# Gram matrix and moments of q and k as blocks of 32 channels on the diagonal, four products at once in strips of array columns

## The chip, the cores and the metric

The kernel runs on one core of a Trainium2 chip, in float32 throughout. The metric is the device time of one execution in microseconds (us). The program is one launch that chains four layers. The change touches only the first part of the first layer, called the preparation, which takes about the first 454 us of the span.

A core has TensorE for matrix products (PE in the profile; its weight loads are listed apart as PEld), VectorE (DVE), ScalarE (ACT), GpSimd (POOL), and SyncE (SP), which issues most of the transfers. TensorE reads SBUF and writes PSUM. A product has a stationary operand, `lhsT`, and a moving operand, `rhs`, and computes `lhsT.T @ rhs`. In this trace each float32 product appears as two passes on PE, each with a weight load of its own on PEld; a transpose appears as one pass.

## The reference

The input `x` has 2 images of 128 channels and 128 x 128 pixels. The first layer is an axial attention along columns, with batch normalisations whose statistics come from the data:

```
x = x + _L0_conv_ref(_gn(x), ...)          # _gn: group norm, groups of 4 channels
...
xg = x.reshape(NW, 8, C // 8, H)            # NW = 2*128 sequences, 8 groups of 16 channels
qkv = einsum('bgch,gdc->bgdh', xg, wg)      # 32 outputs a group: 8 q, 8 k, 16 v
qkv = _bn(qkv, g_qkv, b_qkv, (0, 2), ...)   # moments of each of 256 outputs
q, k, v = qkv[:, :, :8], qkv[:, :, 8:16], qkv[:, :, 16:]
qr = einsum('bgci,cij->bgij', q, q_emb)
kr = einsum('bgci,cij->bgij', k, k_emb).swapaxes(2, 3)
qk = einsum('bgci,bgcj->bgij', q, k)
stacked = _bn(concatenate([qk, qr, kr]), g_sim, b_sim, (0, 2, 3), ...)   # 24 channels
```

The kernel needs the moments of `qkv` and of the three kinds of logits before it can do the attention, and gets them without forming the logits. All of them follow from second moments of channels, and only between channels of one group: the groups of `xg` hold 16 channels each and those of q and of k hold 8 each. So only blocks on the diagonal of each matrix of second moments are used. In `qk` the mean square of the logits is the sum over channel pairs of (second moments of q) times (those of k), sequence by sequence; in `qr` and `kr` it is the sum of second moments at a position times a table made from the embeddings.

## The kernel before

`layer0_prepare` (line 92) has three stages, one after the other. The engines PE, DVE and ACT are driven through `InOrder`, a recorder that keeps the instructions in the order in which the program gives them; all such instructions carry line 81 in the profile, so they are told apart by their tiles. GpSimd and single instructions of the short parts between the stages carry their own lines.

**Gram stage.** `load_image` (line 859) issues 16 transfers of 1 MB on SP, 8 for each image, into `xa[n]` (128 channels on partitions, all pixels of an image behind each other). For every image, 32 steps `t` of 4 image rows follow. `turn(n, t)` transposes the 4 rows (4 transposes of 128 x 128 into one PSUM tile `ps_x`, of which there are three) and copies the result to one of three tiles `xt`, ACT for even `t` and DVE for odd. `xt` has 129 columns per row: 128 channels and a column of ones, so that the product also gives sums. `gather(n, t)` then multiplies each of the 4 turned rows with itself: 4 products with 128 weights and 129 moving columns, all summed in one PSUM tile `gram[n]`. The loop is software-pipelined by one: `turn(t + 1)` is issued ahead of `gather(t)`. Meanwhile GpSimd works through the embedding table (lines 174 to 183), which is needed only in the third stage.

**Between Gram and the second stage** (lines 192 to 301) a serial chain of small instructions on ACT, DVE and PE turns the Gram matrices into group norm scales and the scaled weights `wz`. It uses the whole 128 x 128 matrix `gx` as weights in one product for each image, against weights that are zero outside each channel's own group.

**Second stage, `sequences` and `moments`.** 64 steps, 4 columns of the image each. `sequences(i)` makes q, k and v for 4 columns: 4 products with 128 weights and 256 moving columns into two tiles `ps_zb`; DVE adds the shifts and writes q and k to `zb` (in two blocks, q with 64 channels and k with 64, each with a 65th column of ones) and v to `vs`, which SP stores every fourth step. `moments` of the step before is issued behind that: 8 products with 64 weights and 65 moving columns, written to PSUM partitions 0 to 63 or 64 to 127, so that two neighbours sit in two different halves of the array's columns. ACT copies the q part out (`gq`), DVE multiplies it by the k part, GpSimd adds it to `acc`.

**Third stage, `positions`, `project` and `against_embeddings`.** 32 steps `t` of 4 image rows. `positions(t)`: 8 products with 128 weights and 128 moving columns into two tiles `ps_zt`; DVE writes q and k to `zt`, again in blocks of 65. From `t = 4` on, two or three `project` calls follow (each one product with 512 moving columns into `ps_q`, then two ACT instructions into `sa` and `sb`), and SP stores `sb` (1 MB, tensor `qb_d`) and `sa` (2 MB, `qa_d`) when they are full. `against_embeddings(t - 1)` is last: 16 products with 64 weights and 65 moving columns in the two halves into `pg`; DVE multiplies by the table (`prod`), GpSimd adds to `acc`.

At the end of the second and the third stage a short chain (`logit_scales`) sums `acc` under the mask `strip`. Then `layer0_attention` begins, whose first loads read `qb_d`, `qa_d` and `v_d` back from memory.

The attention itself, which the change does not touch, has products in quarters of the array's columns: `embedded_pe` writes 16 outputs with 32 moving columns to PSUM partitions 0, 32, 64 and 96 in turn (tiles `po<-et,ve`), and `values` does the same with 128 moving columns (`po<-et,vt`).

Of the kernel before, what the change touches and what calls it, by code (L numbers as in the profile page):

```python
# [7 lines left out]
F32 = mybir.dt.float32  # L8
# [7 lines left out]
P = 128  # L16
N = 2
# [74 lines left out]
def layer0_prepare(env, x, prm, mem, alphas):  # L92
# [9 lines left out]
    with ExitStack() as ctx:  # L102
# [13 lines left out]
        with ExitStack() as early:  # L116
# [20 lines left out]

            xt = [wp.tile([P, RT, P + 1], F32, name=f"xt{j}", tag=f"xt{j}") for j in range(3)]
            for t in xt:
                nc.gpsimd.memset(t[:, :, P : P + 1], 1.0)  # L140
            gram = [
                pp.tile([P, P + 1], F32, name=f"gram{n}", tag=f"gram{n}") for n in range(N)
            ]
# [45 lines left out]
            count = float(S * S)  # L189
            gx = wp.tile([P, N, P + 1], F32, name="gx0", tag="gx0")  # L190
            dg = wp.tile([P, P], F32, name="diag", tag="diag")
            mx = wp.tile([P, N, 2], F32, name="mx", tag="mx")
            for n in range(N):
                nc.scalar.mul(gx[:, n], gram[n], 1.0 / count)
                nc.vector.tensor_tensor(dg, gx[:, n, 0:P], env.ident, ALU.mult)
                nc.vector.tensor_reduce(mx[:, n, 1:2], dg, AX.X, ALU.add)
                nc.vector.tensor_copy(mx[:, n, 0:1], gx[:, n, P : P + 1])
            ps = pp.tile([P, 2 * N], F32, name="psg_l0", tag="ps_small")
# [127 lines left out]
        def along(n, k, shape):  # L326
            return (
                rows[:, k, 1 + n, :]
                .rearrange("p (b c) -> p b c", b=(2, NG)[k])
                .unsqueeze(1 if k == 0 else 2)  # L330
                .to_broadcast(shape)
            )
# [3 lines left out]
        onto = kp.tile([P, 1 + N], F32, name="onto", tag="onto")  # L336


        with ExitStack() as part:
            sp = part.enter_context(tc.tile_pool(name="l0s", bufs=1))  # L340
            gp = part.enter_context(tc.tile_pool(name="l0g", bufs=2))
            pp = part.enter_context(tc.tile_pool(name="l0pm", bufs=2, space=PSUM))
            acc = sp.tile([P, 2, 65], F32, name="acc2", tag="acc2")
            nc.gpsimd.memset(acc, 0.0)
            zb = [sp.tile([P, RT, 2, 65], F32, name=f"zb{j}", tag=f"zb{j}") for j in range(2)]
            for t in zb:
                nc.gpsimd.memset(t[:, :, :, 64:65], 1.0)

            def sequences(i, vs):
# [3 lines left out]
                for hf in range(2):  # L353
                    ps = pp.tile([P, 2, 2, P], F32, name="ps_zb", tag="ps_zb", bufs=4)
                    for j in range(2):
# [7 lines left out]
                    dve.tensor_tensor(  # L363
                        z[:, 2 * hf : 2 * hf + 2, :, 0:64],
                        ps[:, :, 0, :].rearrange("p w (b c) -> p w b c", b=2),
                        along(n, 0, [P, 2, 2, 64]),
                        ALU.add,
# [10 lines left out]
            def moments(z):  # L378

                ps = pp.tile([P, 2, 2, 65], F32, name="ps_m", tag="ps_m")  # L380
# [9 lines left out]
                gq = gp.tile([P, 2, 65], F32, name="gq", tag="gq")  # L390
# [23 lines left out]

            tot = sp.tile([P, 65], F32, name="tot2", tag="tot2")
            mom = sp.tile([P, 1, 2], F32, name="mom2", tag="mom2")
            nc.vector.tensor_reduce(tot, acc.rearrange("p a c -> p c a"), AX.X, ALU.add)
            nc.vector.tensor_tensor(tot[:, 0:64], tot[:, 0:64], strip[:, 0:64], ALU.mult)
            nc.vector.tensor_copy(mom[:, 0, 0:1], tot[:, 64:65])
            nc.vector.tensor_reduce(mom[:, 0, 1:2], tot[:, 0:64], AX.X, ALU.add)  # L420
            logit_scales(sp, small, mom, 0, 1)
# [9 lines left out]
        with ExitStack() as part:  # L431
            sp = part.enter_context(tc.tile_pool(name="l0t", bufs=1))
            gp = part.enter_context(tc.tile_pool(name="l0u", bufs=2))
            pp = part.enter_context(tc.tile_pool(name="l0pn", bufs=2, space=PSUM))
            acc = sp.tile([P, RT, 65], F32, name="acc", tag="acc")
            nc.gpsimd.memset(acc, 0.0)
            zt = [sp.tile([P, RT, 2, 65], F32, name=f"zt{j}", tag=f"zt{j}") for j in range(4)]
            for t in zt:
                nc.gpsimd.memset(t[:, :, :, 64:65], 1.0)

            def positions(t):

                zs = []
                for n in range(N):
                    z = zt[2 * (t % 2) + n]
                    ps = pp.tile([P, RT, P], F32, name="ps_zt", tag="ps_zt")
                    for hh in range(RT):
# [7 lines left out]
                    dve.tensor_tensor(  # L455
                        z[:, :, :, 0:64],
                        ps.rearrange("p h (b c) -> p h b c", b=2),
                        along(n, 0, [P, RT, 2, 64]),
                        ALU.add,
# [4 lines left out]
            def against_embeddings(t, zs):  # L464
                pg = pp.tile([P, RT, 65], F32, name="pg", tag="pg")
# [10 lines left out]
                prod = gp.tile([P, RT, 65], F32, name="prod", tag="prod")  # L476
                here = eg[:, :, t * RT : (t + 1) * RT].rearrange("p c i -> p i c")
                dve.tensor_tensor(
                    prod[:, :, 0:64].rearrange("p h (b c) -> p h b c", c=8),
                    pg[:, :, 0:64].rearrange("p h (b c) -> p h b c", c=8),  # L480
                    here[:, :, 0:8].unsqueeze(2).to_broadcast([P, RT, 8, 8]),
                    ALU.mult,
                )
                dve.tensor_tensor(prod[:, :, 64], pg[:, :, 64], here[:, :, 8], ALU.mult)
                nc.gpsimd.tensor_tensor(acc, acc, prod, ALU.add)
# [48 lines left out]

            tot = sp.tile([P, 65], F32, name="tot", tag="tot")
# [3 lines left out]
            nc.vector.tensor_tensor(tot[:, 0:64], tot[:, 0:64], strip[:, 0:64], ALU.mult)  # L539
            for k in range(2):  # L540
                here = slice(64 * k, 64 * k + 64)
                nc.vector.tensor_copy(mom[here, k, 0:1], tot[here, 64:65])
                nc.vector.tensor_reduce(mom[here, k, 1:2], tot[here, 0:64], AX.X, ALU.add)
            logit_scales(sp, small, mom, 1, 2)
# [1533 lines left out]
```

## Time and profile before

| what | value |
|---|---|
| three runs | 5646.67, 5652.51 and 5653.47 us, median 5652.51 |
| the profiled execution | 5645.21 us; its span, first to last instruction, 5643.4 us |
| mean granted TensorE clock | 0.968 of full speed |
| busy over the whole span | PE 5270.7 us (93%), PEld 4712.5, DVE 3697.0 (66%), ACT 2648.5 (47%), POOL 1549.2 (27%) |
| `ps_x`, transposes | 256 passes, the first starts at 6.4 us, the last at 95.6 |
| `gram` products | 512 passes, 9.3 to 97.6 us, median 275 ns each |
| `ps_m`, products of `moments` | 1024 passes, 120.5 to 290.5 us, median 222 ns |
| `ps_zb`, products of `sequences` | 512 passes, 116.7 to 289.2 us, median 383 ns |
| `pg`, products of `against_embeddings` | 1024 passes, 298.5 to 452.9 us, median 222 ns |
| `ps_zt` and `ps_q`, products of `positions` and `project` | 512 passes, median 275 ns, and 128 passes, median 592 ns |

Durations of single passes overlap: passes are pipelined, and one that is listed with 275 ns may be followed by the next after 110 ns. What a block of passes costs is therefore read from the time between the first start of the block and the first start of the block behind it, not from its busy time. The timeline view merges neighbours of one kind into a row: start, time from the first start to the last end, engine, line, operation, tiles, shapes, count, and in brackets the idle time of the engine before the row and what ended it. "128*64 128x65" means 128 rows of the array, 64 weight columns, 65 moving columns. The windows view gives for each stretch: its length, busy time and count of PE, PEld, DVE, ACT and POOL, the granted clock, the share of the DMA engines and GB/s.

### The profile page before, as it was taken

The numbers are of one execution on the slowest core, as the hardware profiler recorded it, in microseconds if no ns is written. First come the engines' busy times: TensorE is split into PE (matmuls) and PEld (weight loads), VectorE is DVE, ScalarE is ACT, GpSimd is POOL, SyncE is SP. The second block draws the span as 40 slices with busy tenths as digits, with TensorE's granted clock in tenths as the row PEclk, the third lists the DMA queues.
The fourth block names the chain that finished last, engine by engine and source line by source line (L and its number), as shares of the span: only waits on it lengthen the run. The fifth ranks groups of instructions, "written<-read, shape, count | busy, mean of one in ns | idle before, by whom it ended". The sixth has DMA issues, their size and how long they took to land. (4 is left out here: it accounts for less than half of the span.)

```text
span 5643.4 us, 164496 instructions
## 1 busy us (share of the span) xinstructions
PE 5270.7 (93%) x68347; PEld 4712.5 (84%) x68347; DVE 3697.0 (66%) x7127; ACT 2648.5 (47%) x7896; POOL 1549.2 (27%) x1169
## 2 busy tenths in 40 slices
PE   8997999999999904999999999999799999999999
PEld 8866888888888704999999999994599999999877
DVE  3645888888888854555555556663466666666698
ACT  1046988898888865443223331003233333333322
POOL 2113666666666622000000002330000000000376
PEclk9998999999999957999999999999899999999999
DMA  3243333333333393000000000103577767777211
GB/s 147 97 186 115 60 59 60 61 62 62 60 60 60 72 377 137 1 1 1 2 1 1 1 1 31 46 24 111 107 88 87 86 90 86 88 89 86 49 50 57
DMA packets 413963, 403.75 MB, mean 72 GB/s; under 512 B 63520, under 2 KB 368544, under 8 KB 402336
## 3 DMA queue, kind: packets, MB, share of 16 engines
q1 hardware_dynamic: 404000, 365.18, 32.0%
q10 hardware_dynamic: 9216, 27.95, 1.3%
q8 instruction: 548, 8.98, 0.7%
q14 instruction: 199, 1.63, 0.1%
HBM read 252.31 MB, written 140.68 MB: 70 GB/s over the span
## 5 line engine op out<-in xcount | busy, mean ns | idle before, releaser
L81 PE MATMUL pl<-ln,wl 128*128 128x128 f32 (+1 forms) x10160 | 1240.6, 276 | 30.5 <-DVE ln L81 30.4
L81 PEld LDWEIGHTS pl<-ln,wl 128*128 128x128 f32 x10160 | 1176.2, 190 | 41.4 <-issue 27.0
L81 ACT ACTIVATE e<-e,mx 128x128 f32<-128x128 f32 x2048 | 793.4, 395 | 0.8 <-DVE mx L81 0.8
L81 ACT COPY sm<-ps_s 128x432 f32<-128x432 f32 (+1 forms) x768 | 318.4, 487 | 801.5 <-PE ps_s L81 801.5
L81 POOL TENSOR_TENSOR e<-e,total 128x1024 f32<-128x1024 f32 x256 | 485.9, 1898 | 476.0 <-DVE total L81 465.5
L81 ACT COPY res<-ln 128x128 f32<-128x128 f32 x762 | 262.3, 344 | 719.2 <-DVE ln L81 719.2
L81 PE MATMUL ps_s<-s,xw 100*128 100x144 f32 x4096 | 546.4, 287 | 0.6 <-ACT sm L81 0.6
L81 POOL TENSOR_TENSOR res<-ln,x1t 128x128 f32<-128x128 f32 x256 | 134.4, 525 | 1494.1 <-DVE ln L81 1494.1
L81 DVE COPY s<-ps_w 100x1152 f32<-100x1152 f32 x256 | 346.4, 1353 | 301.7 <-PE ps_w L81 301.7
L81 PE MATMUL po<-sm,wdef 128*128 128x256 f32 x2304 | 539.1, 379 | 0.0
L81 PE MATMUL pl<-ln,ws 128*128 128x128 f32 x4064 | 536.8, 273 | 0.0
L81 POOL COPY et<-et 128x1024 f32<-128x1024 f32 x256 | 516.9, 2019 | 35.3 <-DVE et L81 27.1
L81 PEld LDWEIGHTS ps_s<-s,xw 100*128 100x128 f32 x4096 | 518.2, 191 | 1.1 <-ACT sm L81 1.1
L81 DVE TENSOR_TENSOR v<-pl,c 128x128 f32<-128x128 f32 x508 | 148.1, 291 | 538.4 <-PE pl L81 538.4
L81 PEld LDWEIGHTS pl<-ln,ws 128*128 128x128 f32 x4064 | 494.5, 190 | 0.0
L81 ACT ACTIVATE r<-gen,alphas 128x1536 f32<-128x1536 f32 x256 | 395.0, 1543 | 171.5 <-PE gen L81 142.7
L81 PEld LDWEIGHTS po<-sm,wdef 128*128 128x128 f32 x2304 | 419.8, 190 | 47.6
L81 POOL MEMSET col<- 128x10 f32 (+1 forms) x72 | 5.9, 122 | 1477.4 <-DVE res L81 1469.9
L81 ACT ACTIVATION_READ_ACCUMULATOR e<-e,mx 128x1 f32 x2048 | 396.1, 193 | 0.0
L81 DVE SCALAR_TENSOR_TENSOR ln<-v,res 128x128 f32<-128x128 f32 x1016 | 343.5, 338 | 49.2 <-DVE v L81 1.2
L81 PE MATMUL te<-cst_main,e 128*128 128x128 f32 x2048 | 338.5, 288 | 24.5 <-POOL e L81 17.3
L81 DVE COPY et<-te 128x512 f32<-128x512 f32 x512 | 348.1, 680 | 11.5 <-PE te L81 10.9
(241 smaller groups left out, 9351.8 us busy)
## 6 DMA issues: line engine op xcount, KB each, us to landing
xw<-px_d SPq DMA_DIRECT2D x1280, 80.0 KB
xa<-in_x SPq DMA_DIRECT2D x16, 1024.0 KB
v_d<-vs SPq DMA_DIRECT2D x16, 1024.0 KB
qb_d<-sb SPq DMA_DIRECT2D x16, 1024.0 KB
qa_d<-sa SPq DMA_DIRECT2D x8, 2048.0 KB
zz<-qb_d SPq DMA_DIRECT2D x1024, 16.0 KB
vt<-v_d SPq DMA_DIRECT2D x64, 256.0 KB
qk<-qa_d SPq DMA_DIRECT2D x256, 64.0 KB
```

What stands on the lines that cost most here:

```text
L81: return lambda *a, **k: self.tc.keep_in_program_order(issue(*a, **k))
```

## The change

All three kinds of second moments are formed in blocks of 32 channels. Tiles that had 1 block of 129 (`xt`) or 2 of 65 (`zb`, `zt`) columns per row get 4 blocks of 33, each with 32 channels and a column of ones. Every product has 32 weights and 33 moving columns and writes to PSUM partitions 0, 32, 64 or 96, that is to one of four strips of the array's columns, and neighbours in the program go to different strips. `gram[n]` is then 128 x 33: the four diagonal blocks below each other. `gather` issues 16 products in place of 4, `moments` 16 in place of 8, `against_embeddings` 32 in place of 16. In `moments` a strip stands for a column of the pair and a block: the columns of a pair and the two halves of q lie in the four strips, and those of k in a second slice of the same tile.

What reads the results is adapted: the diagonal is taken with `eye`, a 128 x 32 mask; `gd` spreads the four blocks back into a 128 x 128 matrix with zeros outside them, by means of the mask `own0`, since the next product needs the full form as weights; `strip32` replaces `strip` for the sums. `eye`, `own0` and `strip32` are three short DVE instructions that stand ahead of the first `xt` copy in DVE's order; `gd` is one DVE instruction for each image, between the copy of the sums and the reduction of the diagonal. The PSUM tiles keep the banks that they had; the order of instructions on SP, ACT and POOL is the same, with smaller shapes.

```diff
-            xt = [wp.tile([P, RT, P + 1], F32, name=f"xt{j}", tag=f"xt{j}") for j in range(3)]
+            xt = [wp.tile([P, RT, 4, 33], F32, name=f"xt{j}", tag=f"xt{j}") for j in range(3)]
...
-                copy(to[:, :, 0:P], ps)
+                copy(to[:, :, :, 0:32], ps.rearrange("p r (s c) -> p r s c", s=4))
...
                 for r in range(RT):
-                    pe.matmul(
-                        gram[n],
-                        lhsT=xr[:, r, 0:P],
-                        rhs=xr[:, r, :],
-                        start=(t == 0 and r == 0),
-                        stop=(t == NT - 1 and r == RT - 1),
-                    )
+                    for s in range(4):
+                        pe.matmul(
+                            gram[n][32 * s : 32 * s + 32],
+                            lhsT=xr[:, r, s, 0:32],
+                            rhs=xr[:, r, s, :],
+                            start=(t == 0 and r == 0),
+                            stop=(t == NT - 1 and r == RT - 1),
+                        )
...
+            nc.vector.tensor_reduce(eye, blocks.rearrange("p s c -> p c s"), AX.X, ALU.add)
+            nc.vector.tensor_reduce(own, blocks, AX.X, ALU.add)
...
-                nc.vector.tensor_tensor(dg, gx[:, n, 0:P], env.ident, ALU.mult)
+                nc.vector.tensor_tensor(dg, gx[:, n, 0:32], eye, ALU.mult)
...
+                nc.vector.tensor_tensor(
+                    gd[:, n],
+                    gx[:, n, 0:32].unsqueeze(1).to_broadcast([P, 4, 32]),
+                    own.unsqueeze(2).to_broadcast([P, 4, 32]),
+                    ALU.mult,
+                )
...
-                nc.tensor.matmul(pt, lhsT=gx[:, n, 0:P], rhs=wn[n], start=True, stop=True)
+                nc.tensor.matmul(
+                    pt,
+                    lhsT=gd[:, n].rearrange("p s c -> p (s c)"),
...
+        strip32 = kp.tile([P, 32], F32, name="strip32", tag="strip32")
+        nc.vector.tensor_tensor(strip32, strip[:, 0:32], strip[:, 32:64], ALU.add)
...
-                for w in range(RT):
+                ps = pp.tile([P, 2, 2, 33], F32, name="ps_m", tag="ps_m")
+                for half in range(2):
                     for b in range(2):
-                        pe.matmul(
-                            ps[64 * (w % 2) : 64 * (w % 2) + 64, w // 2, b, :],
-                            lhsT=z[:, w, b, 0:64],
-                            rhs=z[:, w, b, :],
-                            start=True,
-                            stop=True,
-                        )
+                        for s in range(4):
+                            w, block = 2 * half + s // 2, 2 * b + s % 2
+                            pe.matmul(
+                                ps[32 * s : 32 * s + 32, half, b, :],
+                                lhsT=z[:, w, block, 0:32],
+                                rhs=z[:, w, block, :],
+                                start=True,
+                                stop=True,
+                            )
...
-                        for b in range(2):
+                        for b in range(4):
                             pe.matmul(
-                                pg[64 * b : 64 * b + 64, hh, :],
-                                lhsT=zs[n][:, hh, b, 0:64],
+                                pg[32 * b : 32 * b + 32, hh, :],
+                                lhsT=zs[n][:, hh, b, 0:32],
                                 rhs=zs[n][:, hh, b, :],
```

The DVE additions that fill `zb` and `zt`, and those that use `gq`, `prod`, `acc` and `tot`, follow with runs of 32 in place of 64 and rows of 33 in place of 65.

More of the change, by code (lines that the diff above doesn't have):

```diff
@@ L135, in layer0_prepare @@
             gqkv, bqkv = vecs[:, 0:2], vecs[:, 2:4]
-            xt = [wp.tile([P, RT, P + 1], F32, name=f"xt{j}", tag=f"xt{j}") for j in range(3)]
+            xt = [wp.tile([P, RT, 4, 33], F32, name=f"xt{j}", tag=f"xt{j}") for j in range(3)]
             for t in xt:
[L140 to L143, printed above, removed]
+                nc.gpsimd.memset(t[:, :, :, 32:33], 1.0)
+            gram = [pp.tile([P, 33], F32, name=f"gram{n}", tag=f"gram{n}") for n in range(N)]
             for n in range(N):
@@ L189, in layer0_prepare @@
             count = float(S * S)
-            gx = wp.tile([P, N, P + 1], F32, name="gx0", tag="gx0")
-            dg = wp.tile([P, P], F32, name="diag", tag="diag")
+            gx = wp.tile([P, N, 33], F32, name="gx0", tag="gx0")
+            gd = wp.tile([P, N, 4, 32], F32, name="gd0", tag="gd0")
+            dg = wp.tile([P, 32], F32, name="diag", tag="diag")
+            eye = wp.tile([P, 32], F32, name="eye", tag="eye")
+            own = wp.tile([P, 4], F32, name="own0", tag="own0")
+            blocks = env.ident.rearrange("p (s c) -> p s c", s=4)
+            nc.vector.tensor_reduce(eye, blocks.rearrange("p s c -> p c s"), AX.X, ALU.add)
+            nc.vector.tensor_reduce(own, blocks, AX.X, ALU.add)
             mx = wp.tile([P, N, 2], F32, name="mx", tag="mx")
@@ L194, in layer0_prepare @@
                 nc.scalar.mul(gx[:, n], gram[n], 1.0 / count)
-                nc.vector.tensor_tensor(dg, gx[:, n, 0:P], env.ident, ALU.mult)
+                nc.vector.tensor_tensor(dg, gx[:, n, 0:32], eye, ALU.mult)
                 nc.vector.tensor_reduce(mx[:, n, 1:2], dg, AX.X, ALU.add)
-                nc.vector.tensor_copy(mx[:, n, 0:1], gx[:, n, P : P + 1])
+                nc.vector.tensor_copy(mx[:, n, 0:1], gx[:, n, 32:33])
+                nc.vector.tensor_tensor(
[4 more added lines that the diff above has]
+                )
             ps = pp.tile([P, 2 * N], F32, name="psg_l0", tag="ps_small")
@@ L235, in layer0_prepare @@
                 pt = pp.tile([P, 256], F32, name="pt", tag="pt")
-                nc.tensor.matmul(pt, lhsT=gx[:, n, 0:P], rhs=wn[n], start=True, stop=True)
+                nc.tensor.matmul(
+                    pt,
+                    lhsT=gd[:, n].rearrange("p s c -> p (s c)"),
+                    rhs=wn[n],
+                    start=True,
+                    stop=True,
+                )
                 wg = wp.tile([P, 256], F32, name=f"wg{n}", tag=f"wg{n}")
@@ L328, in along @@
                 rows[:, k, 1 + n, :]
-                .rearrange("p (b c) -> p b c", b=(2, NG)[k])
+                .rearrange("p (b c) -> p b c", b=(4, NG)[k])
                 .unsqueeze(1 if k == 0 else 2)
@@ L342, in layer0_prepare @@
             pp = part.enter_context(tc.tile_pool(name="l0pm", bufs=2, space=PSUM))
-            acc = sp.tile([P, 2, 65], F32, name="acc2", tag="acc2")
+            acc = sp.tile([P, 2, 33], F32, name="acc2", tag="acc2")
             nc.gpsimd.memset(acc, 0.0)
-            zb = [sp.tile([P, RT, 2, 65], F32, name=f"zb{j}", tag=f"zb{j}") for j in range(2)]
+            zb = [sp.tile([P, RT, 4, 33], F32, name=f"zb{j}", tag=f"zb{j}") for j in range(2)]
             for t in zb:
-                nc.gpsimd.memset(t[:, :, :, 64:65], 1.0)
+                nc.gpsimd.memset(t[:, :, :, 32:33], 1.0)
             def sequences(i, vs):
@@ L363, in sequences @@
                     dve.tensor_tensor(
-                        z[:, 2 * hf : 2 * hf + 2, :, 0:64],
-                        ps[:, :, 0, :].rearrange("p w (b c) -> p w b c", b=2),
-                        along(n, 0, [P, 2, 2, 64]),
+                        z[:, 2 * hf : 2 * hf + 2, :, 0:32],
+                        ps[:, :, 0, :].rearrange("p w (b c) -> p w b c", b=4),
+                        along(n, 0, [P, 2, 4, 32]),
                         ALU.add,
@@ L378, in moments @@
             def moments(z):
-                ps = pp.tile([P, 2, 2, 65], F32, name="ps_m", tag="ps_m")
-                for w in range(RT):
+                ps = pp.tile([P, 2, 2, 33], F32, name="ps_m", tag="ps_m")
+                for half in range(2):
                     for b in range(2):
-                        pe.matmul(
-                            ps[64 * (w % 2) : 64 * (w % 2) + 64, w // 2, b, :],
-                            lhsT=z[:, w, b, 0:64],
-                            rhs=z[:, w, b, :],
-                            start=True,
-                            stop=True,
-                        )
-                gq = gp.tile([P, 2, 65], F32, name="gq", tag="gq")
+                        for s in range(4):
[4 more added lines that the diff above has]
+                                rhs=z[:, w, block, :],
+                                start=True,
+                                stop=True,
+                            )
+                gq = gp.tile([P, 2, 33], F32, name="gq", tag="gq")
                 act.copy(gq, ps[:, :, 0, :])
@@ L413, in layer0_prepare @@
                     z_last = z
-            tot = sp.tile([P, 65], F32, name="tot2", tag="tot2")
+            tot = sp.tile([P, 33], F32, name="tot2", tag="tot2")
             mom = sp.tile([P, 1, 2], F32, name="mom2", tag="mom2")
             nc.vector.tensor_reduce(tot, acc.rearrange("p a c -> p c a"), AX.X, ALU.add)
-            nc.vector.tensor_tensor(tot[:, 0:64], tot[:, 0:64], strip[:, 0:64], ALU.mult)
-            nc.vector.tensor_copy(mom[:, 0, 0:1], tot[:, 64:65])
-            nc.vector.tensor_reduce(mom[:, 0, 1:2], tot[:, 0:64], AX.X, ALU.add)
+            nc.vector.tensor_tensor(tot[:, 0:32], tot[:, 0:32], strip32, ALU.mult)
+            nc.vector.tensor_copy(mom[:, 0, 0:1], tot[:, 32:33])
+            nc.vector.tensor_reduce(mom[:, 0, 1:2], tot[:, 0:32], AX.X, ALU.add)
             logit_scales(sp, small, mom, 0, 1)
@@ L434, in layer0_prepare @@
             pp = part.enter_context(tc.tile_pool(name="l0pn", bufs=2, space=PSUM))
-            acc = sp.tile([P, RT, 65], F32, name="acc", tag="acc")
+            acc = sp.tile([P, RT, 33], F32, name="acc", tag="acc")
             nc.gpsimd.memset(acc, 0.0)
-            zt = [sp.tile([P, RT, 2, 65], F32, name=f"zt{j}", tag=f"zt{j}") for j in range(4)]
+            zt = [sp.tile([P, RT, 4, 33], F32, name=f"zt{j}", tag=f"zt{j}") for j in range(4)]
             for t in zt:
-                nc.gpsimd.memset(t[:, :, :, 64:65], 1.0)
+                nc.gpsimd.memset(t[:, :, :, 32:33], 1.0)
             def positions(t):
@@ L455, in positions @@
                     dve.tensor_tensor(
-                        z[:, :, :, 0:64],
-                        ps.rearrange("p h (b c) -> p h b c", b=2),
-                        along(n, 0, [P, RT, 2, 64]),
+                        z[:, :, :, 0:32],
+                        ps.rearrange("p h (b c) -> p h b c", b=4),
+                        along(n, 0, [P, RT, 4, 32]),
                         ALU.add,
@@ L464, in against_embeddings @@
             def against_embeddings(t, zs):
-                pg = pp.tile([P, RT, 65], F32, name="pg", tag="pg")
+                pg = pp.tile([P, RT, 33], F32, name="pg", tag="pg")
                 for hh in range(RT):
                     for n in range(N):
-                        for b in range(2):
+                        for b in range(4):
                             pe.matmul(
-                                pg[64 * b : 64 * b + 64, hh, :],
-                                lhsT=zs[n][:, hh, b, 0:64],
+                                pg[32 * b : 32 * b + 32, hh, :],
+                                lhsT=zs[n][:, hh, b, 0:32],
                                 rhs=zs[n][:, hh, b, :],
@@ L475, in against_embeddings @@
                             )
-                prod = gp.tile([P, RT, 65], F32, name="prod", tag="prod")
+                prod = gp.tile([P, RT, 33], F32, name="prod", tag="prod")
                 here = eg[:, :, t * RT : (t + 1) * RT].rearrange("p c i -> p i c")
                 dve.tensor_tensor(
-                    prod[:, :, 0:64].rearrange("p h (b c) -> p h b c", c=8),
-                    pg[:, :, 0:64].rearrange("p h (b c) -> p h b c", c=8),
-                    here[:, :, 0:8].unsqueeze(2).to_broadcast([P, RT, 8, 8]),
+                    prod[:, :, 0:32].rearrange("p h (b c) -> p h b c", c=8),
+                    pg[:, :, 0:32].rearrange("p h (b c) -> p h b c", c=8),
+                    here[:, :, 0:8].unsqueeze(2).to_broadcast([P, RT, 4, 8]),
                     ALU.mult,
                 )
-                dve.tensor_tensor(prod[:, :, 64], pg[:, :, 64], here[:, :, 8], ALU.mult)
+                dve.tensor_tensor(prod[:, :, 32], pg[:, :, 32], here[:, :, 8], ALU.mult)
                 nc.gpsimd.tensor_tensor(acc, acc, prod, ALU.add)
@@ L533, in layer0_prepare @@
                 zs_last = zs
-            tot = sp.tile([P, 65], F32, name="tot", tag="tot")
+            tot = sp.tile([P, 33], F32, name="tot", tag="tot")
             mom = sp.tile([P, 2, 2], F32, name="mom", tag="mom")
@@ L538, in layer0_prepare @@
             nc.vector.tensor_reduce(tot, acc.rearrange("p a c -> p c a"), AX.X, ALU.add)
-            nc.vector.tensor_tensor(tot[:, 0:64], tot[:, 0:64], strip[:, 0:64], ALU.mult)
+            nc.vector.tensor_tensor(tot[:, 0:32], tot[:, 0:32], strip32, ALU.mult)
             for k in range(2):
                 here = slice(64 * k, 64 * k + 64)
-                nc.vector.tensor_copy(mom[here, k, 0:1], tot[here, 64:65])
-                nc.vector.tensor_reduce(mom[here, k, 1:2], tot[here, 0:64], AX.X, ALU.add)
+                nc.vector.tensor_copy(mom[here, k, 0:1], tot[here, 32:33])
+                nc.vector.tensor_reduce(mom[here, k, 1:2], tot[here, 0:32], AX.X, ALU.add)
             logit_scales(sp, small, mom, 1, 2)
```

## The prediction

> **What bounds the kernel now.** I read the windows of the three stages first, then the timeline inside each, then the place in the attention where the same kind of product already runs.
>
> ```profile
> 20.00:97.60 77.60, 77.31 (x691) 76.60 (x689) 20.62 (x32) 16.73 (x29) 25.72 (x7) 1.00 0.36 148
> 98.00:116.60 18.60, 10.52 (x30) 6.84 (x30) 8.83 (x50) 2.81 (x6) 0.00 (x0) 0.63 0.00 0
> 116.70:291.20 174.50, 173.99 (x1536) 155.27 (x1536) 115.26 (x321) 17.20 (x64) 29.23 (x66) 1.00 0.27 92
> 293.40:454.00 160.60, 154.98 (x1666) 111.29 (x1665) 67.22 (x138) 83.69 (x129) 23.40 (x37) 1.00 0.47 194
> 600.00:650.00 50.00, 49.47 (x1267) 41.76 (x1267) 43.55 (x62) 44.98 (x172) 34.65 (x18) 1.00 0.35 65
> ```
>
> In all three stages PE is busy for nearly the whole stretch at the full clock, while DVE, ACT and the DMA engines (share 0.27 to 0.47) have room. What shortens a stage's PE work shortens the span, until something else takes over. The last line is a stretch of the attention, for comparison. Inside the stages:
>
> ```profile
> 19.72 0.60 PE L81 MATMUL ps_x<-cst_main,xa 128*128 128x128 f32 x4
> 20.15 1.06 PE L81 MATMUL gram<-xt 128*128 128x129 f32 x8
> 20.43 0.69 DVE L81 COPY xt<-ps_x 128x512 f32<-128x512 f32 x1 [1.97 <-PE ps_x L81]
> 21.05 0.60 PE L81 MATMUL ps_x<-cst_main,xa 128*128 128x128 f32 x4
> ...
> 202.27 0.73 PE L81 MATMUL ps_m<-zb 128*64 128x65 f32 x16
> 202.93 2.13 PE L81 MATMUL ps_zb<-wz,xa 128*128 128x256 f32 x8
> ...
> 381.97 1.15 PE L81 MATMUL pg<-zt 128*64 128x65 f32 x32
> 383.06 2.05 PE L81 MATMUL ps_zt<-wz,xa 128*128 128x128 f32 x16
> ```
>
> From start to next start: a Gram step is 1.33 us, 0.43 of transposes and 0.90 of products; a `moments` block is 202.93 - 202.27 = 0.66; a `pg` block is 383.06 - 381.97 = 1.09.
>
> **The nearest rows for the new products.** The attention has products in four strips, with 16 weights and 32 moving columns, and transposes between blocks in strips:
>
> ```profile
> 699.12 0.63 PE L81 MATMUL te<-cst_main,e 128*128 128x128 f32 x4
> 699.68 0.63 PE L81 MATMUL po<-et,vt 128*16 128x128 f32 x16
> 701.76 0.73 PE L81 MATMUL po<-et,ve 128*16 128x32 f32 x64
> 702.42 0.66 PE L81 MATMUL te<-cst_main,e 128*128 128x128 f32 x4
> 702.91 1.04 PE L81 MATMUL lg<-cst_main,r 128*128 128x128 f32 x8
> ...
> L81 PE MATMUL po<-et,ve 128*16 128x32 f32 x16384 | 194.9, 197 | 25.7 <-issue 20.1 <-ACT svt L81 3.4 <-ACT ste L81 2.1
> ```
>
> 64 passes take 0.66 us. The row ends at 701.76 + 0.73 = 702.49 and one pass is listed with 197 ns, so the last began at 702.29: 63 intervals in 0.53 us, a pace of 8.4 ns, then 0.13 us until the next kind starts. The same reckoning on `pg` (222 ns a pass): 31 intervals in 0.93 us, a pace of 30 ns, then 0.16. So one strip repeats every 2 x 30 = 60 ns with 64 weights and 65 columns, and every 4 x 8.4 = 34 ns with 16 weights and 32 columns. The new pass has 32 weights and 33 columns. No row has 32 weights with a short moving operand in four strips. Its pace lies between 8.4 ns and 60 / 4 = 15 ns, the case in which four strips share what two strips share now: a round holds 4 x 32 = 128 weight columns, as 2 x 64 does today. I take 8.4: in `pg` one pass takes 60 ns for 65 columns, so with half the weights and half the columns it should need about the 34 ns that the 32-column row shows.
>
> The Trainium skill speaks against the change here: TensorEngine Tiling, section Instruction Overhead, gives each matmul an overhead of about 60 cycles and warns against tiling a dimension that is already small, and TensorE: Matmul & The Clock Gate (Part 1) puts the least start-to-start distance at about 25 ns. At 25 ns a pass the three stages would lose about 45 us together; the row above has 8.4 ns, so the case goes by the row.
>
> **Part by part.**
> - *Gram.* 32 passes: 31 x 8.4 ns + 0.13 = 0.39 us, in place of 0.90. The transposes now stand between blocks in strips; such a block took 699.68 - 699.12 = 0.56 us, and 702.91 - 702.42 = 0.49 where the next was a full one, against 0.43 now. Step: 0.56 + 0.39 = 0.95, less by 0.38. Of the 64 steps 61 run at the pace above (16.2 to 97.6 us): 23 us. The copies come close to it: DVE's starts 0.71 us after the transposes start and takes 0.69, ready at 1.40, with the longer transposes about 1.5; the products want it at 0.95 + 0.56 = 1.51. I take off 1 us: 22. The loads do not hold it: 1 MB feeds 4 steps, 3.8 us, and the DMA engines moved over 400 GB/s until about 45 us, 2.6 us a load.
> - *Moments.* 32 passes, 0.39 in place of 0.66, the switch from full products being there already: 0.27 x 64 = 17.3 us. DVE is busy 115 of 174 us and stays under the new 157.
> - *Third stage.* 64 passes, 0.66 in place of 1.09: 0.43 x 32 = 13.8 us. ACT is busy 84 of 161 us. SP's stores leave with `sa` and `sb`, so their last landing, for which the attention waits (POOL's memset of `zz` started only 10.98 us after its previous work, released by `qb_d<-sb`), moves along with the stage. The shorter `acc` and `tot` at the end lie under that landing and count nothing.
> - *Small instructions.* DVE and ACT write the same number of elements in runs of 32; DVE's `vs`, which writes runs of 16, took 414 ns against 425 for `zb` with runs of 64, so nothing. `eye`, `own0` and `strip32` lie before DVE's first copy at 8.33 us, waiting for `cst_main` and `late` (ACT's first work was released by `late` at 7.25 us); without that cover about 0.7 us. In the chain from 98 to 116.6 us `gd` stands ahead of the reduction, 0.2 us, against a smaller scaling, product and reduction: nothing net.
> - *Instruction supply.* The three stages issue 64 x 72 + 64 x 80 + 32 x 160 + 64 x 4 = 15,100 passes and loads, about 7,200 more than before. The window 600 to 650 holds 2 x 1267 of them and 10 instruction packets: 253 a packet, so 60 packets. In the attention PE sometimes stopped inside a block in strips with nothing to wait for:
>
> ```profile
> 724.47 0.65 PE L81 MATMUL po<-et,ve 128*16 128x32 f32 x55
> 726.12 0.26 PE L81 MATMUL po<-et,ve 128*16 128x32 f32 x9 [1.01 <-issue]
> ```
>
> These stops add up to 20.1 us (the group row above) over some 306 packets (2534 per 50 us over 1530 us, by 253): 0.066 us a packet, 4 us for 60. The bounds are 0 and, at 1.01 us for each, 60. The skill's Runtime: NRT & Kernel Launch, section Instruction fetch mechanics, calls the crossing of a 16 KiB block mostly hidden, which would make this term about zero; the row shows that it is not always.
>
> Sum: 22 + 17.3 + 13.8 - 4 = 49 us less. The profiled execution took 5645.2, so 5596 by its own account; it is 7 us below the median of the runs, 5652.5, which gives 5603. I predict 5602.
>
> **Rivals.**
> - *The pace is 15 ns* (strips share loads or reads). Blocks of 0.60 and 1.08 us: Gram 61 x 0.17 = 10.4, moments 64 x 0.06 = 3.8, third stage nothing; less the 4, about 10 us gained: 5642. For it: equal weight columns in a round. Against it: `po<-et,vt`, four strips with 128 moving columns each, took 0.56 us for 16 passes, 35 ns each, less than half of what 128-column passes take in one.
> - *Supply holds the Gram stage.* It asks for 72 passes and loads in 0.95 us, 76 per us against 51 in the attention, while loads fill the DMA engines. Then Gram gains nothing: 5652.5 - 31 + 4 = 5625. Against it: blocks in the attention run 128 of them in 0.66 us, mostly without a stop.
> - *Four strips do not overlap with 32 weights*, so that each pass waits for the one before in any strip: 34 ns, the repeat of a single strip. Gram 0.56 + 31 x 0.034 + 0.13 = 1.74, 61 x 0.41 = 25 us more; moments 1.18, 33 more; third stage 2.27, 38 more; with the 4, 100 us: 5752. It turns the sign from a pace of about 17 ns on (103.6 us to gain at no pace at all, less 5.89 us for each ns of it, less 4). For it: twice to four times as many instructions, which the sum depends on. Against it: 8.4 ns in the attention and two strips that overlap today.
>
> **How the numbers follow.** The forecast has a chance of 0.70, the pace of 15 ns 0.10, the supply rival 0.10, no overlap 0.08, no effect 0.02. Less than 0.2%, 11 us, can't be told from no change. Faster: 0.70 + 0.10 and most of the pace rival, 0.88; same 0.03; slower 0.09. Low end: transposes at 0.49, no waits for copies or supply, 27 + 17 + 14 = 58 us, and from the lower runs 5584. High end: the pace rival, 5642. The forecast's own range is 5584 to 5620.
>
> **What would show it.** Right: start-to-start blocks of about 0.39 us for `gram` and `ps_m` and 0.66 for `pg`, a Gram stage that ends at about 75 us, stages two and three 17 and 13 us shorter, and an unchanged attention. Wrong: idle PE inside blocks put down to issue, waits of PE for `xt`, a granted clock below 1.00 in the stages, or blocks with 15 to 34 ns a pass.

## The result, and the profile after

| | median of the runs | lowest and highest | ratio to before, 95% interval |
|---|---|---|---|
| before (4 runs beside it) | 5649.59 us | 5646.45 to 5653.47 | |
| after (4 runs) | 5617.97 us | 5610.16 to 5624.39 | 0.9944 [0.9932, 0.9956] |

The change gains 31.6 us where 49 were forecast. The profiled execution of after took 5624.39 us, the slowest of the four (span 5622.6), that of before 5645.21, faster than all four in the table. So the two spans differ by only 20.8 us. The preparation alone shows more: the last `pg` pass ended at 453.1 us and now ends at 423.3, 29.8 us earlier. From there to the end ten profiles (before, after and the kernels below, which share that part of the program) took 5189 to 5204 us, before 5190 and after 5199. The eight of them that have the new second and third stages already range over all of this, so the 9 us between before and after can't be read as an effect of the change.

The windows of after, with the same columns as above and boundaries at the new stage ends; the third line is the first one's part under the loads, the fourth its part behind them:

```profile
20.00:91.70 71.70, 60.09 (x2009) 46.73 (x2008) 19.92 (x32) 16.07 (x28) 25.79 (x7) 0.90 0.40 163
91.70:111.80 20.10, 11.93 (x32) 7.38 (x31) 8.88 (x51) 2.85 (x6) 0.00 (x0) 0.53 0.00 1
...
20.00:45.00 25.00, 18.82 (x540) 14.61 (x540) 5.36 (x8) 4.11 (x7) 24.53 (x7) 0.80 1.01 417
55.00:91.00 36.00, 33.70 (x1241) 26.36 (x1227) 12.93 (x22) 10.19 (x18) 0.00 (x0) 1.00 0.02 5
...
111.80:271.30 159.50, 159.01 (x2560) 140.84 (x2560) 109.71 (x321) 13.86 (x64) 20.62 (x66) 0.98 0.30 101
273.10:424.00 150.90, 145.61 (x2690) 102.26 (x2689) 60.26 (x138) 83.97 (x129) 14.88 (x38) 0.98 0.51 208
```

The second and third stages are 15 and 9.5 us shorter, where 17.3 and 13.8 were forecast. The Gram stage is only 6 us shorter (its end went from 97.8 to 91.7 us; 22 were forecast). PE is no longer busy all through it: 60.09 of 71.70 us, where it was 77.31 of 77.60, and the granted clock fell from 1.00 to 0.90. Under the loads, while the DMA share is 1.01, PE started 540 passes and 540 weight loads in 25 us, 43 instructions per us; behind them 2468 in 36 us, 69 per us. The timeline of PE in after, inside that stretch:

```profile
20.00 0.46 PE L81 MATMUL gram<-xt 128*32 128x33 f32 x32
20.39 0.66 PE L81 MATMUL ps_x<-cst_main,xa 128*128 128x128 f32 x4
20.98 0.34 PE L81 MATMUL gram<-xt 128*32 128x33 f32 x17
23.94 0.33 PE L81 MATMUL gram<-xt 128*32 128x33 f32 x15 [2.61 <-issue]
24.20 0.66 PE L81 MATMUL ps_x<-cst_main,xa 128*128 128x128 f32 x4
24.79 0.67 PE L81 MATMUL gram<-xt 128*32 128x33 f32 x32
25.39 1.12 PE L81 MATMUL ps_x<-cst_main,xa 128*128 128x128 f32 x4
26.43 0.67 PE L81 MATMUL gram<-xt 128*32 128x33 f32 x32
...
32.93 0.38 PE L81 MATMUL gram<-xt 128*32 128x33 f32 x20
36.03 0.44 PE L81 MATMUL gram<-xt 128*32 128x33 f32 x12 [2.72 <-issue]
...
201.28 0.46 PE L81 MATMUL ps_m<-zb 128*32 128x33 f32 x32
201.67 2.13 PE L81 MATMUL ps_zb<-wz,xa 128*128 128x256 f32 x8
...
379.95 0.77 PE L81 MATMUL pg<-zt 128*32 128x33 f32 x64
380.64 2.05 PE L81 MATMUL ps_zt<-wz,xa 128*128 128x128 f32 x16
```

A whole block of 32 passes takes 20.39 - 20.00 = 0.39 us, and a step 20.98 - 20.00 = 0.98. But the next block stops after 17 passes for 2.61 us with nothing that it waits for, and behind the stop the clock is halved: transposes take 1.04 us to the next start in place of 0.59. Another stop, of 2.72 us, splits a later block after 20 passes. The blocks of the other two stages are whole: 0.39 us for `ps_m`, 0.69 for `pg`. The tile view of `gram`, for PE alone, adds up its idle time before these passes by what ended it, and counts the places:

```profile
  issue: 10.0, 6
  ACT xt L81: 1.0, 2
  DVE xt L81: 0.8, 2
```

In before it has no line for issue, and neither view shows a wait of weight for `xt`. While the loads run, the timeline shows five stops of 0.77, 2.61, 0.85, 2.72 and 2.99 us (the first ahead of a transpose, the last begun shortly before the loads end at about 47 us), together 9.9. Put beside the instruction packets that the trace records (queue q8, 16 KB each), they line up:

| packet starts | PE goes on | stop | passes and weight loads before it |
|---|---|---|---|
| 15.22 | 17.64 | 0.77 | 449 |
| 21.40 | 23.94 | 2.61 | 706 |
| 27.68 | 30.00 | 0.85 | 961 |
| 33.64 | 36.03 | 2.72 | 1218 |
| 46.08 | 48.66 | 2.99 | 1730 |

The stops lie a multiple of 256 instructions apart, and PE goes on 2.3 to 2.6 us after a packet has started. While the loads run the packets are 6.0 to 6.3 us apart (the one at 39.75, ahead of no stop, is left out of the table), behind them 3.85 on average.

### The profile page after: what moved, and what is told of

Same layout as the page of the kernel before. It is cut to its first block, busy times and chain, and to the rows that moved or that the text cites. A ratio compares the mean times of both kernels' runs of the same rounds, so it can differ in the third digit from the quotient of the medians.

```text
span 5622.6 us, 171669 instructions
## 1 busy us (share of the span) xinstructions
PE 5229.8 (93%) x71931; PEld 4656.8 (83%) x71931; DVE 3685.4 (66%) x7132; ACT 2652.3 (47%) x7896; POOL 1530.1 (27%) x1169
## 5 line engine op out<-in xcount | busy, mean ns | idle before, releaser
L81 PE MATMUL te<-cst_main,e 128*128 128x128 f32 x2048 | 337.8, 287 | 27.1 <-POOL e L81 20.1
```

Source lines behind the costliest of these rows:

```text
L81: return lambda *a, **k: self.tc.keep_in_program_order(issue(*a, **k))
```

## The experiments

All medians of the first four are compared with 15 runs of the kernel before, median 5651.91 us, those of the last four with 9 runs, median 5650.82. The ratios stand as they were recorded and are not exactly the quotients of the medians (for e1 that would be 0.9950). "Gram" is the end of the last `gram` pass, "second" and "third" the first starts of `ps_zb` and `ps_zt`, "pg" the end of the last `pg` pass, all in the profiled execution.

| kernel | median, runs | ratio to before | Gram | second | third | pg |
|---|---|---|---|---|---|---|
| before | | | 97.8 | 116.7 | 293.4 | 453.1 |
| after | 5617.97, 4 | 0.9944 [0.9932, 0.9956] | 91.7 | 111.8 | 273.1 | 423.3 |
| e1: Gram stage of before | 5623.49, 5 | 0.9943 [0.993, 0.9957] | 96.9 | 115.8 | 274.7 | 425.1 |
| e2: new Gram stage alone | 5645.71, 11 | 0.9992 [0.9983, 1.0001] | 91.9 | 111.5 | 290.5 | 450.6 |
| e3: Gram in blocks of 64 | 5615.82, 5 | 0.9939 [0.9925, 0.9953] | 87.3 | 107.0 | 267.9 | 416.5 |
| e4: one image loaded first | 5613.67, 1 | | 83.0 | 103.0 | 263.8 | 412.7 |
| e5: Gram products twice | 5682.4, 1 | | 148.8 | 167.5 | 326.5 | 476.6 |
| e6: blocks of 64, then of 32 | 5609.8, 5 | 0.9928 [0.9914, 0.9941] | 82.5 | 102.5 | 263.1 | 412.3 |
| e7: e6 with filled gaps | 5601.94, 5 | 0.9914 [0.99, 0.9927] | 82.0 | 97.3 | 256.3 | 404.4 |
| e8: after again | 5617.7, 5 | 0.9943 [0.9929, 0.9957] | 91.5 | 111.3 | 272.1 | 420.3 |

**e1 and e2: the two halves of the change alone.** e1 takes the Gram stage of before into the changed kernel, e2 the new Gram stage into the kernel before:

```diff
 # e1, against after
-            xt = [wp.tile([P, RT, 4, 33], F32, name=f"xt{j}", tag=f"xt{j}") for j in range(3)]
+            xt = [wp.tile([P, RT, P + 1], F32, name=f"xt{j}", tag=f"xt{j}") for j in range(3)]
...
-                    lhsT=gd[:, n].rearrange("p s c -> p (s c)"),
...
+                nc.tensor.matmul(pt, lhsT=gx[:, n, 0:P], rhs=wn[n], start=True, stop=True)
 # e2, against before: the same lines the other way
```

> Gram stage with one block of 129 columns as before, second and third stage in strips of 32. Theory A (PE's instruction supply: 256 instructions per fetch, about 6.1 us a fetch while the loads fill the DMA engines and 3.75 us later, against a demand of 72 in 0.98 us in the changed Gram stage): the Gram stage has no idle time by issue and ends at 97.5 to 98 us as before; second and third stage keep their gain of 15 + 10 us, so about 5649.6 - 25 to - 29 = 5621 to 5625 us, at most some 6 us slower than the changed kernel. Rival (the new Gram stage is worth its 22 us in most runs and the profile caught a bad one): about 5649.6 - 29 = 5621 here, but the changed kernel would then have to measure near 5600.

> Gram stage in strips of 32, second and third stage as before. Theory A: idle by issue of 20 us or more in the Gram stage, which ends near 90 us; total 2 to 8 us less than before, 5642 to 5648 us. If the working of the prediction held for this stage: 22 us less, 5628 us, Gram stage over at 75 us.

The tile view of `gram` for PE, of e1 and then of e2, by what ended PE's idle time:

```profile
  ACT xt L81: 1.0, 2
...
  issue: 9.8, 6
  ACT xt L81: 1.1, 2
  DVE xt L81: 0.5, 1
```

The stage of before in e1 has no stops (its tile view has no line for issue) and ends at 96.9 us; stages two and three still gain, 28 us by the medians. The new stage alone in e2 stops as in after (issue 9.8 us in 6 places and 1.1 ahead of a transpose, where 20 or more were expected), ends at 91.9 and gains 6 us, with an interval that just reaches 1. So the Gram stage's gain goes missing in the Gram stage itself and does not hang on the two stages behind it.

**e3: fewer instructions in the Gram stage.** Two blocks of 64 in place of four of 32, 40 passes and weight loads a step in place of 72:

```diff
-            xt = [wp.tile([P, RT, 4, 33], F32, name=f"xt{j}", tag=f"xt{j}") for j in range(3)]
+            xt = [wp.tile([P, RT, 2, 65], F32, name=f"xt{j}", tag=f"xt{j}") for j in range(3)]
...
-                    for s in range(4):
+                    for s in range(2):
...
-                            gram[n][32 * s : 32 * s + 32],
-                            lhsT=xr[:, r, s, 0:32],
+                            gram[n][64 * s : 64 * s + 64],
+                            lhsT=xr[:, r, s, 0:64],
```

> Gram stage in two blocks of 64 (8 products of 64 weights and 65 columns a step, 40 passes and loads), the rest as in the changed kernel. Theory A: 40 instructions a step of 0.56 + 15 x 0.03 + 0.05 + 0.16 = 1.2 us is 33 to 35 per us, under the 42 per us that the loaded supply gave, so no idle by issue and full clock throughout; the stage ends at 86 to 90 us in every run, total 5649.6 - 9 - 27 = 5610 to 5616 us, equal to or faster than the changed kernel and with less scatter. Rival (the stops come with every switch between full products and strips, not with the number of instructions): the same number of switches, so the same idle time, and a stage of 91 + 15 = 106 us.

A window and two rows of the timeline of e3:

```profile
20.00:87.30 67.30, 66.45 (x1114) 53.27 (x1112) 19.99 (x32) 16.04 (x28) 25.97 (x7) 1.00 0.42 172
...
22.49 0.69 PE L81 MATMUL gram<-xt 128*64 128x65 f32 x16
23.11 0.66 PE L81 MATMUL ps_x<-cst_main,xa 128*128 128x128 f32 x4
```

A block costs more array time, 0.62 us in place of 0.39, and yet the stage ends 4.4 us earlier than in after: 33 instructions per us are less than the 43 that came through under the loads, no stop is put down to issue, and the clock stays at 1.00.

**e4: the same instructions without transfers.** Only image 0 is loaded ahead of the Gram stage. Both halves of the stage work on image 0, so the statistics of image 1 come from image 0; image 1 is loaded behind the stage (the small copy into `xa[1]` makes its load wait for the Gram sums):

```diff
-            for n in range(N):
-                load_image(nc, xa[n], x, n)
+            load_image(nc, xa[0], x, 0)
...
-                    pe.transpose(ps[:, r, :], xa[n][:, t * RT + r, :], env.ident)
+                    pe.transpose(ps[:, r, :], xa[0][:, t * RT + r, :], env.ident)
...
+            nc.vector.tensor_copy(xa[1][:, 0:S:16, 0:1], gx[:, 1, 0:8].unsqueeze(2))
+            load_image(nc, xa[1], x, 1)
```

> The changed kernel with the loads of the second image moved behind the Gram stage; both halves of the stage work on the first image (its statistics stand in for those of the second, so the output differs). The DMA engines are full until about 27 us instead of 45. Theory A: after 27 us a fetch takes 3.75 us, stops by issue shrink from 0.9 to 3.0 us to under 0.7 us each and the half clock behind them is gone; the stage ends at 79 to 84 us instead of 91.7. Rival (a stop at every 256 instructions whatever the transfers): stops of 0.8 to 3 us go on after 27 us and the stage ends at 90 to 93 us.

Windows of e4 ahead of and behind the end of its loads, and a row of its timeline:

```profile
9.00:27.00 18.00, 13.97 (x396) 10.81 (x396) 3.93 (x6) 3.20 (x6) 13.01 (x4) 0.93 1.02 418
28.00:83.00 55.00, 52.01 (x1868) 40.35 (x1868) 18.53 (x30) 14.89 (x26) 18.44 (x5) 1.00 0.02 6
...
24.32 0.33 PE L81 MATMUL gram<-xt 128*32 128x33 f32 x15 [2.61 <-issue]
```

With the same order of PE instructions as after, the two stops ahead of 27 us are there (1.01 and 2.61 us) and the long later ones are not: none over 0.63. The packets stand 3.73 us apart on average as soon as the loads end, PE gets 3736 instructions in 55 us, 68 per us, and the stage ends at 83.0 in place of 91.7. A cost of the strips, or of crossing 256 instructions as such, would have stayed.

**e5: the supply by itself.** Every product of the Gram stage is issued twice:

```diff
-                    for s in range(4):
+                    for s in (0, 1, 2, 3, 0, 1, 2, 3):
...
```

> The changed kernel with every strip product of the Gram stage issued twice, so that a step has 136 passes and weight loads in place of 72; the Gram sums, and with them the statistics, are twice as large. If the supply of PE's instructions sets the pace (256 passes and loads per 3.75 us when the DMA engines are free, per about 6.1 us while the image loads fill them): 136 / 68.3 = 2.0 us a step behind the loads and about 3.2 us ahead of their end at about 45 us, Gram stage over at about 150 us. If a pass costs only the array's time and the stops come from something else in the stage: 0.56 + 0.66 = 1.22 us a step, stage over at about 95 to 105 us.

```profile
20.00:44.90 24.90, 15.47 (x475) 12.32 (x474) 2.07 (x3) 1.76 (x3) 24.43 (x7) 0.52 1.02 419
55.00:145.00 90.00, 63.15 (x3106) 50.86 (x3107) 15.76 (x26) 13.71 (x24) 0.00 (x0) 1.00 0.02 5
...
121.09 0.27 PE L81 MATMUL gram<-xt 128*32 128x33 f32 x8
122.39 0.70 PE L81 MATMUL gram<-xt 128*32 128x33 f32 x56 [1.03 <-issue]
```

Two windows of e5, under and behind the loads, and a stop in its timeline. The stage ends at 148.8 us. Behind the loads, with the DMA engines idle (share 0.02) and the clock at 1.00, PE got 6213 instructions in 90 us: 69 per us, the same as in after and in e4 although a block has twice as many. The stops behind the loads are 0.6 to 1.6 us in every 256 instructions, where after and e4 have 0.2 to 0.6 at some of them, and the packets are 3.73 us apart on average as in e4: the stop takes up what is left of that time, so it is a rate, and not a fixed price of a crossing. Under the loads the rate was 38 per us, at a clock of 0.52.

**e6: each half of the stage as its supply allows.** Image 0, whose steps run while the loads do, in two blocks of 64, image 1 in four of 32:

```diff
+            BLK = (64, 32)
...
-                    for s in range(4):
+                    for s in range(P // c):
                         pe.matmul(
-                            gram[n][32 * s : 32 * s + 32],
-                            lhsT=xr[:, r, s, 0:32],
+                            gram[n][c * s : c * s + c],
+                            lhsT=xr[:, r, s, 0:c],
```

Here `c` is `BLK[n]`, and `xt`, `eye` and `own` exist once for each block size.

> The changed kernel with image 0 of the Gram stage in two blocks of 64 (40 passes and loads a step) and image 1 in four blocks of 32 (72 a step). If the loads of the images slow the supply, image 0, which runs while they do, has no long stops, and image 1, which runs behind them, goes at 72 / 68.3 = 1.05 us a step: Gram stage over at 79 to 82 us, where two blocks of 64 for both images ended at 87.3 and the changed kernel at 91.7; about 5 to 8 us under two blocks of 64 throughout, 5608 to 5611 us, ratio to the kernel before 0.992 to 0.993. If strips of 32 stop PE whatever else runs, image 1 loses about 8 us again: stage over at 88 or later.

```profile
9.00:50.00 41.00, 40.60 (x640) 32.64 (x640) 11.13 (x21) 9.54 (x17) 32.41 (x8) 1.00 0.95 392
50.00:82.30 32.30, 31.01 (x1144) 24.07 (x1144) 10.97 (x16) 8.85 (x16) 0.00 (x0) 1.00 0.02 5
```

In the windows of e6, image 0 runs on under loads at 392 GB/s, and image 1 takes 32.3 us for 32 steps, 1.01 us each, 71 instructions per us. The stage ends at 82.5, a little behind the expected 79 to 82, and the kernel is 7.9 us under the changed one run beside it (5609.8 against 5617.7).

**e7: the clock between the stages.** In after the granted clock was 0.50 from 93.1 to 116.9 us and again from 274.0 to 280.8, both times into the next stage; the windows of after at the starts of the second and third stages have it (the column ahead of the DMA share):

```profile
111.80:116.90 5.10, 5.10 (x12) 4.08 (x13) 1.69 (x5) 0.00 (x0) 0.26 (x3) 0.50 0.00 0
274.00:280.80 6.80, 6.03 (x47) 5.51 (x49) 3.18 (x11) 0.21 (x1) 0.43 (x6) 0.50 0.12 40
```

e7 is e6 with transposes that nothing reads, in the places where PE waits:

```diff
+            def warm(k):
+                ps = pp.tile([P, RT, P], F32, name="ps_x", tag="ps_x", bufs=3)
+                for i in range(k):
+                    nc.tensor.transpose(ps[:, i % RT, :], env.ident, env.ident)
+
+            warm(7)
...
+            warm(14)
...
+            warm(28)
...
+                nc.tensor.transpose(idle[:, 0:P], env.ident, env.ident)
```

> The mixed kernel with idle PE filled by transposes whose results nothing reads, in the chain between the Gram stage and the second stage and in the wait ahead of the third. If the half clock at the starts of stages two and three comes from the idle PE between the stages, the clock stays at 1.0: the chain of 20 us gets 3 to 5 us shorter (its products run at full clock), stage two saves about 2.5 us at its start and stage three 2 to 3.4: 7 to 10 us under the mixed kernel. If the clock falls for another reason (the stops of the Gram stage, or work between the stages), the half clock stays and the time is that of the mixed kernel or above it.

The chain between the stages in e6, then the same in e7 with the stage behind it, as windows of each, and rows of the timeline of e7:

```profile
82.50:102.50 20.00, 11.86 (x30) 7.30 (x30) 8.80 (x51) 2.85 (x6) 0.00 (x0) 0.58 0.00 1
102.50:260.00 157.50, 157.47 (x2507) 139.85 (x2511) 108.47 (x317) 13.32 (x62) 20.39 (x65) 0.99 0.31 102
```

```profile
82.00:97.30 15.30, 13.06 (x93) 10.26 (x88) 8.76 (x51) 2.85 (x6) 0.00 (x0) 1.00 0.01 1
97.30:253.20 155.90, 155.85 (x2507) 138.94 (x2511) 108.51 (x318) 13.32 (x62) 20.39 (x65) 1.00 0.31 103
...
88.66 3.04 PE L229 MATMUL ps_x<-cst_main 128*128 128x128 f32 x26
92.23 0.58 PE L342 MATMUL psq<-cols,ct 128*128 128x3 f32 x4 [0.54 <-DVE cols L313]
...
92.81 1.46 PE L328 MATMUL psr<-dgs,late 128*128 128x384 f32 x4
```

The clock stays at 1.00 from 12.8 us on through all three stages. The four `psr` passes take 1.46 us where after's row had 2.91, the chain falls from 20.0 to 15.3 us, the second stage from 157.5 to 155.9, and from the third stage's first pass to the last `pg` it is 148.1 us in place of 149.2. Of the three savings expected, that of the chain came (4.7 us), and those of the second stage (1.6 us against about 2.5) and of the third (1.1 against 2 to 3.4) were too high. The last `pg` ends 7.9 us earlier, and the median is 7.9 us lower: 5601.94, 0.9914 of before and 15.8 us under the changed kernel, the fastest that was run.

**e8: the changed kernel again.**

> The changed kernel itself beside the mixed kernel and the one with filled gaps, on the same chip: Gram stage over at about 91.7 us with stops of 2.3 to 3 us at multiples of 256 PE instructions, ratio to the kernel before about 0.994. If the stops were an accident of the first profile, they are absent and the stage ends at about 80 us.

The stops of 1.36, 2.61, 2.42, 0.65 and 2.72 us are again 256 or 512 instructions apart, under the loads; the stage ends at 91.5 us and the ratio is 0.9943. They belong to the kernel, not to one execution.

## Why the prediction was half right

- **Sign: right; mechanism: right in the second and third stages.** Each stage of before was bound by PE, and shorter blocks shorten it. 5618 lies in the range and within the forecast's own one, but it is nearer to the supply rival's 5625 than to the 5602 forecast, and two of the prediction's own signs of being wrong are there: idle PE inside blocks put down to issue, and a granted clock below 1.00 (0.90 in the Gram stage, 0.98 in the other two). The low end of the range, 5584, is 3 us under its own sum (5645.2 - 58 = 5587); nothing rests on it.
- **Pace of the strips: right.** 8.4 ns a pass was forecast from `po<-et,ve`; `gram` and `ps_m` blocks take 0.39 us as computed, and neighbours inside a `ps_m` block start 8.6 ns apart on average. In `pg` a block is 0.696 us, 9.0 ns a pass, 0.036 us more than forecast, 1.2 us over 32 steps. The rivals of 15 and of 34 ns fall with these rows, and the 25 ns a pass that the prediction set beside the row is not in them either.
- **Transposes between strips: 0.59 us** where 0.56 was taken; 0.03 x 61 = 1.8 us of the Gram stage.
- **Moments: 17.3 forecast, 15 measured, 17 with the clock held** (from the first to the last `ps_zb` it took 172.9 us before and 155.9 in e7). What was missing is 2.5 us in the first stretch of the stage, 5.1 us at half clock. Before, the clock had been back at full at 114.1 us, ahead of the stage; after, the chain runs at half clock from 1.4 us behind the Gram stage (before, 2.7) and until 5.1 us into the next one. The chain itself became 1.2 us longer (18.8 to 20.1).
- **Third stage: 13.8 forecast, 9.5 measured in the first profile, 11.5 in e8 and 11.6 in e7.** In the first profile the half clock lasted 6.8 us at its start and cost 2.0 us against e8, where it lasted 3.4 and cost nothing against e7 (PE waits there for DVE's `zt` anyway, 1.05 us in before, 0.77 in after). The pace of `pg` is another 1.2; the last 1 us was not looked for.
- **Instruction supply: the term of the sum that was mis-sized.** The prediction put 4 us on it, 0.066 us for each of 60 packets, from the attention's stops. In the Gram stage alone it took 9.9 us of stops, and behind three of them 13.6 us ran at half clock, 6.8 us more: 16.7 us together. From the forecast end of about 75 us to the measured 91.7 there are as many, but that the two agree so closely is chance: the transposes (1.8) and three short stops behind the loads (1.4) come on top, the two steps by which after was ahead at 16.2 us (five `gram` blocks done where before had three, about 1.9 us) go off, and half-clock stretches hold waits too, so the account is good to some 2 us. The rival that named this got the place right and asked for the whole Gram gain; 6 of 22 us were left. What was said against it, that the attention runs 128 instructions in 0.66 us mostly without a stop, compared a burst with a rate: over 50 us the attention asks for 51 a us, which is below the 68 to 71 that e4, e5 and e6 got with idle DMA engines, while the new step asks for 74, and under the loads only 38 to 43 came. The average was in the same paragraph (76 against 51) and would have served as the test: demand of a stage over time against the rate that a stage with full queues has ever had.
- The Trainium skill, Runtime: NRT & Kernel Launch, section Instruction fetch mechanics, takes the fetch to be mostly hidden. That agrees with e1 and e3 (18 and 33 instructions per us, no long stop) and not with after, e4 and e5, where the measured rate decides.

The loads lengthen one part of a packet's cycle alone. At the stops of after, e4 and e5 PE goes on 2.2 to 2.9 us after a packet has started, under the loads as behind them; from there to the start of the next packet it is 3.2 to 4.1 us under the loads and mostly 1.0 to 1.2 (at most 1.8) behind them. A packet itself takes about 1.0 us under the loads and 0.9 to 1.5 behind them. So under loads a packet waits longer before it starts; where it waits, in the DMA engines' rings or at the memory, was not tried.

## What to carry to other kernels

When a change replaces large products by many small ones, set the PE instructions that a stage asks for per us (passes and loads) against the rate at which they can be supplied, and for stages under heavy loading take the lower rate: here 68 to 71 per us with free DMA engines and 38 to 43 with full ones. Where the demand is above it, a coarser split that costs more array time can be faster (two blocks of 64 ended the Gram stage 4.4 us earlier than four of 32, though the medians of the whole kernel, 5615.8 and 5618.0 us, are too close to tell), and the split may differ between the half of a stage that runs under the loads and the half that does not. A stop or a dependent chain also costs what the half clock takes from the work behind it, and transposes that nothing reads can buy that back.

## What the runs showed of the hardware that was not expected

- PE's instructions come in packets of 16 KB for 256 instructions, and in a stage that asks for more than they bring, the packets set the pace: 3.73 us apart on average with idle DMA engines (e4 and e5), 5.9 to 6.5 us under loads of about 420 GB/s (after, e2, e5 and e8).
- Inside the Gram stage of after, e2, e4 and e8 the granted clock fell to 0.50 behind PE stops of 2.3 to 3.0 us, for 3.4 to 6.8 us, and not behind stops up to 1.4 us. Every half-clock stretch that was listed (3.4, 6.8, 13.7, 20.5 and 23.9 us) is a multiple of about 3.4 us, as a free-running window would make it; the Trainium skill, TensorE: Matmul & The Clock Gate, Part 1, describes such a window of that length. Such a window would also make the same wait of 2.03 us ahead of the third stage end in 6.8 us of half clock in one profile of after and 3.4 in the other, and one of 2.46 us in before in none; where the window stood was not measured.
- Four strips of 32 x 33 run at 8.6 ns a pass (9.0 in `pg`), but 4 full transposes between them cost 0.59 us in place of 0.43.
